# Four edits to a fused transformer and mixture-of-experts kernel: the order of its first two attentions, the router constants, the rotation rows, and the first norm of five batches

## The chip, the cores and the metric

The kernel runs on one core of one Trainium2 chip. A time is the device time of one execution in microseconds (us); medians are over several timed runs. The profile is of one further execution, taken by the hardware profiler. Engines are named as in the profile: PE is TensorE's matmul, PEld its weight load, DVE VectorE, ACT ScalarE, POOL GpSimd, SP SyncE.

## The reference

The input `x` is 8 batches of 256 tokens with 256 channels in float32; `cond_256` is a condition vector of 64 numbers for each batch, and `mask` a row of masked keys. Four layers follow, each added to its input:

```
# layer 0: attention with 16 heads, then a gated feed-forward of 1024 hidden channels
norm(x, t, ...) = (t @ gw.T + gb) * x * rsqrt(mean(x*x) + 1e-6) + (t @ bw.T + bb)
x1 = x + attention(norm1(x), Wq, Wk, Wv, Wo)
x  = x + x1 + (silu(norm2(x1) @ gate_w.T) * (norm2(x1) @ hid_w.T)) @ out_w.T
# layer 1: masked attention, then an RMS norm scaled and shifted by silu(cond) @ Wc.T + bc
x  = x + modulated_rmsnorm(masked_attention(x))
# layer 2: a spectral gate that is constant over frequency, then quaternion products: a 4x4 mix
#          for each of 64 positions of the channel group ("rotation")
x  = x + rotate(x * gate)
# layer 3: 8 experts of three matrices, the 2 best for each token, weighed by a softmax
gate = (rms_w * x * rsqrt(mean(x*x) + 1e-6)) @ wg_W + wg_b + (cond @ gg_W + gg_b)
x  = x + sum over the top 2 experts of weight * expert(x)
```

The factor and the offset of layer 0's norms depend on the batch and the channel alone, and the last bracket of the router's `gate` ("router constants") on the batch and the expert alone.

## The kernel before

A batch of 256 tokens lies as two tiles of 128 tokens; `NQ` is 2, and `KC` is the 2 chunks of 128 channels. The work of layers 0 and 1 runs batch by batch; the experts follow, in tiles of tokens that are gathered by expert.

**Order.** TensorE's instructions run in the order of the program's text throughout (`manual_schedule`), VectorE's and ScalarE's until the experts, GpSimd's during the first twelve attention blocks. SyncE, which issues most loads, is put in order by the framework's scheduler. A block (`block`) is one of an attention's four pieces: the scores of a chunk of heads `c` against a half of the keys `kc` (`s_a`, four matmuls over 32 rows), and one exponential on ScalarE (`pe_a`). There is one buffer of scores in PSUM, so the next scores wait for the exponential. Every second block also multiplies with the values (`values`, `o_a`); VectorE then turns the sums (`tu_a`), divides them and turns them again (`oT_a`). After the second such piece `after_first` projects them out (`py`, which reads `oT_a`), adds the input and starts the second norm.

`run` plays a string of blocks. Beside each block it takes pieces from a generator until the assumed costs reach the block's gap (a piece is 1.9 if it says nothing else; a "break" ends the block's pieces), calls what a finished attention has left over (`then`, after at most `soon` further pieces), and at the block's end one step of the generators given in `beside`. `others(b)` yields the feed-forward of batch `b` (`swiglu`: turns of the second norm, groups `pg` and `ph`, then `pd`), mixed with the first operands of batch `b + 3` (`first`) and the operands of its second attention. For batch 0 its first piece, the turns, is followed by a "break".

**First norm of a batch.** `first_norm` squares on ScalarE, takes the reciprocal root on VectorE in eleven small instructions (`rsqrt`), and multiplies the token-major rows on GpSimd (`xs_n`). `first` then has TensorE turn them (`flipped`, four transposes into `pt_n`), and VectorE evicts them with factor and offset (`xT_n`, through `conditioned`).

**Router constants.** `set_up_router` multiplies the condition, repeated for 128 rows, with `ggw`: one matmul of 8 columns for each batch (`pgconst`).

**Rotation.** `prepare_quaternions` normalizes and lays out the quaternions (VectorE, then 32 small copies on GpSimd into `lm` and `rm`), `prepare_rotation` multiplies them, `set_up_rotation` spreads the sixteen coefficients of each position over all partitions: diagonal matrices on VectorE (`diag`), two matmuls with ones (`pcoef`), copies on ScalarE (`coef`). It is a generator; `second_step` plays it in steps, one for each of five blocks.

**The head.** TensorE first multiplies the identity with itself (`keep_busy`, `pw`) while the first batch is loaded and squared. `set_up_factors(j0)` makes factors and offsets of a norm with eight small matmuls (`paff`); before, those of the first norm are made in the head and those of the second beside the first block.

PSUM tiles tagged "m" (projections, turns, `py`, feed-forward) share three banks.

Of the kernel before, what the change touches and what calls it, by code (L numbers as in the profile page):

```python
# [8 lines left out]
F32 = mybir.dt.float32  # L9
# [9 lines left out]
C = 64  # L19
# [474 lines left out]
def block_kernel(ctx: ExitStack, tc: tile.TileContext, a: dict, out: bass.AP):  # L494
# [10 lines left out]
    tokens_r = tokens[0:T, :].rearrange("(q p) c -> p q c", p=P)  # L505
    mod_rows = dram.tile([B, 2 * D], F32, tag="mod_rows", name="mod_rows")

    slots = dram.tile([TABLE, 4], I32, tag="slots", name="slots")
# [69 lines left out]
    first_factors, second_factors = slice(0, 2), slice(2, 4)  # L578
    nc.sync.dma_start(out=aff_w[:, first_factors, :], in_=a["aff_w"][:, first_factors, :])
    wk0 = load_w(nc.sync, "L0_WkT", D, D, pool_a)  # L580
# [4 lines left out]
    wo0 = load_w(nc.sync, "L0_WoT_turned", D, D, pool_a)  # L585
    nc.sync.dma_start(out=aff_w[:, second_factors, :], in_=a["aff_w"][:, second_factors, :])
    gate_w = load_w(nc.sync, "gate_wT", D, HID, pool_b)
# [158 lines left out]
    def prepare_router():  # L746
        cond_b = pool_b.tile([C, B, P], F32, tag="hT", bufs=1, name="cond_b")
        nc.vector.tensor_copy(cond_b, condT[0:C, :].unsqueeze(2).to_broadcast([C, B, P]))

        for k in range(KC):  # L750
            nc.vector.tensor_scalar(wgs[:, k, :], wg[:, k, :], rmsw[:, k : k + 1], None, ALU.mult)
        nc.vector.tensor_tensor(gb_b, wgb_b, ggb_b, ALU.add)
        nc.vector.tensor_copy(rank, ranki)
        return cond_b

    def set_up_router(cond_b):
        pg = ps_m.tile([P, B, E], F32, tag="m", name="pgconst")
        for b in range(B):
            nc.tensor.matmul(pg[:, b, :], cond_b[:, b, :], ggw, start=True, stop=True)
        nc.vector.tensor_tensor(gconst, pg, gb_b.unsqueeze(1).to_broadcast([P, B, E]), ALU.add)  # L760
        yield 0.4
# [35 lines left out]
    def set_up_rotation():  # L797
# [16 lines left out]

        diag = []
        for n in range(2):
            d = work.tile([C, 2, 4, C], F32, tag="x3", bufs=2, name=f"diag_{n}")
            for i in range(2):
                nc.vector.tensor_tensor(
                    d[:, i], ident[0:C, 0:C].unsqueeze(1).to_broadcast([C, 4, C]),  # L820
                    rotg[0:C, :, 2 * n + i : 2 * n + i + 1].to_broadcast([C, 4, C]), ALU.mult,
                )
            diag.append(d)
        yield
        for n in range(2):
            pc = bank(f"pcoef_{n}", (P, 2 * 4 * C))
            nc.tensor.matmul(
                pc, ones[0:C, :], diag[n].rearrange("p i j c -> p (i j c)"), start=True, stop=True
            )
            nc.scalar.copy(coef[:, 2 * n : 2 * n + 2], pc)  # L830

# [6 lines left out]
        )  # L838
        scaled = work.tile([P, KC, B, E], F32, tag="r_msg", bufs=1, name="scaled")
        nc.vector.tensor_tensor(  # L840
# [30 lines left out]
    def bank(name, shape=(P, 2, S)):  # L871
        return ps_m.tile(list(shape), F32, tag="m", name=name)
# [165 lines left out]
    def do(parts):  # L1038
        for _ in parts:
            pass  # L1040
# [5 lines left out]
    def first_norm(b):  # L1046
# [5 lines left out]
        )  # L1052

    def first(b):

        s = state[b]
        xT = conditioned(
            s.pop("xs1"), b, 0, f"n1_{b}", (nc.vector, nc.vector if b else nc.scalar), apart=b == 0
        )
        yield 0.6  # L1060
        s["qkv0"] = yield from qkv(xT, wq0, wk0, wv0, f"a0_{b}")
# [705 lines left out]

    def keep_busy(n, name):

        pw = bank(name, (P, P))  # L1770
        for _ in range(n):
            nc.tensor.matmul(pw, ident, ident, start=True, stop=True)

    by_text = {mybir.EngineType.DVE, mybir.EngineType.Activation, mybir.EngineType.Pool}
    with tc.manual_schedule(engines=by_text):
        keep_busy(9, "pw0")
        n1 = first_norm(0)
        next(n1)
        next(n1)
        set_up_factors(0)  # L1780
        do(n1)
        keep_busy(4, "pw1")
        g0 = first(0)
        next(g0)
        keep_busy(3, "pw2")
        scales()
        do(first_norm(1))
        for _ in g0:
            pass
        blank = set_up_slots()  # L1790
        prepare_condition()
        cond_b = prepare_router()
        finish_slots(*blank)
        def factors():
            set_up_factors(2)
            yield 0.4

        def third(b):

            operand = first(b)  # L1800
            yield next(operand)
            yield from set_up_router(cond_b)
            yield from operand

        operands = chain(set_up_condition(), factors(), first(1))
        run("b", operands, 1.4, rest=False)
        run("bbb", operands, 1.9, {1: [at_once(first_norm(2))]})
        operands = third(2)
        run("bb", operands, [1.0, 3.8], rest=False)

        def second_step():
            set_up_rows()
            prepare_quaternions()
            yield
            rotation = set_up_rotation()
            next(rotation)
            yield
            next(rotation)
            yield
            do(first_norm(3))  # L1820
            next(rotation)
            set_up_ones()
            yield
            yield from rotation

        set_up = second_step()
        run("bbbbbb", chain(operands, others(0)), 7.2, {n: [set_up] for n in range(5)})
    by_text = {mybir.EngineType.DVE, mybir.EngineType.Activation}
# [3 lines left out]
    for i in range(2, B - 1):  # L1832

        placed = {
            2: lambda: once(compare_queries), 4: lambda: at_once(place_choices(0)),
            6: lambda: at_once(place_choices(1)),
        }.get(i, lambda: iter(()))()
        last, rotated = rotated, rotate(i - 2)
        n1 = first_norm(i + 2) if i + 2 < B else iter(())
        n2, r1 = in_parts(i, "n2"), in_parts(i - 2, "r1")  # L1840
        gaps = [7.6, 5.7, 3.8, 5.7, 8.2, 3.8, 2.5, 3.8] if i + 2 < B else [7.6, 3.8, 1.9, 5.7, 7.6, 1.2, 1.9, 3.8]
        starts = {0: [last], 1: [last, n2], 2: [n2, n1]}
        beside = {
            0: [last], 1: [last, n2], 2: [n1, n1], 3: [last], 4: [placed], 5: [r1], 6: [rotated],
            7: [rotated, rotated],
        }
        if i == B - 2:

            early = table("early", (NG - 2) * NTG, EARLY, ALU.is_ge)
            for t in (4, 7):  # L1850
                beside[t].append(early)
        run("bbbbbbbb", others(i - 1), gaps, beside, late_=() if i + 2 < B else (4,), starts=starts)
# [12 lines left out]
    n2 = in_parts(B - 1, "n2")  # L1865
    run("bbbvn", pieces, 3.8, {0: [n2], 2: [early], 3: [early]}, soon=2, rest=False, starts={0: [n2], 1: [n2]})

# [192 lines left out]
```

## Time and profile before

| what | value |
|---|---|
| median of 3 timed runs | 710.83 us (710.71 to 712.07) |
| the profiled execution's own time | 712.39 us |
| its span, first to last instruction | 710.7 us |
| mean granted TensorE clock | 0.995 |
| busy share of PE, PEld, DVE, ACT, POOL | 98%, 76%, 52%, 36%, 26% |
| first scores of attention a0_0, a0_2, a1_0 | 16.46, 58.57, 99.38 us |
| TensorE's own idle time by the waits, 0 to 130 us | 1.5 us at the start, 0.4 later |

Lines of a timeline read: start, length, engine, line of the kernel, instruction, output and inputs, shape, how many in a row; in brackets the idle time before and what ended it. Lengths of matmuls overlap, since they are pipelined: the cost of a group in a row is the distance from its start to the next group's start. Lines of the windows read: stretch, its length, then busy time and number of instructions of PE, PEld, DVE, ACT and POOL, the granted clock of TensorE, the share of the DMA engines, and GB/s.

### The profile page before, as it was taken

The page shows a single profiled execution, that of the slowest core. Times are in us where ns is not written, and L with a number is a line of the kernel's source. Part 1 is how long each engine was busy: PE and PEld are TensorE (multiplying, and loading weights), DVE is VectorE, ACT ScalarE, POOL GpSimd, SP SyncE. Part 2 cuts the span into 40 slices and gives each one's busy share as a digit, 9 for nine tenths or more (in the row PEclk, how much of TensorE's full clock was granted, in tenths as well). Part 3 has the DMA queues.
Part 4 walks back from the last instruction along what each step waited for, and adds up shares of the span by engine and source line. Part 5 has one row for each costly group of instructions (what it writes and reads, how often), then busy time and mean ns, then how long its engine had stood idle before and what let it go on. Part 6 is the DMA issues. An engine that isn't in the chain of part 4 may idle for free.

```text
span 710.7 us, 11254 instructions
## 1 busy us (share of the span) xinstructions
PE 698.1 (98%) x4300; PEld 538.6 (76%) x4300; DVE 368.1 (52%) x1175; ACT 256.4 (36%) x412; POOL 182.2 (26%) x222
## 2 busy tenths in 40 slices
PE   9999999999999999999999999999999999999995
PEld 8567776766766767766666786788888998999894
DVE  4547445485477585477585686688421222222221
ACT  3653334354364354264444235422221212222120
POOL 5302500100100140100140016323464432352213
PEclk9999999999999999999999999999999999999999
DMA  8500000000011000001000050827675867586722
GB/s 284 177 17 0 16 1 16 1 16 16 1 56 35 1 17 1 0 21 54 2 17 1 16 201 11 305 88 242 155 251 159 251 224 220 152 262 206 247 32 30
DMA packets 26495, 67.52 MB, mean 95 GB/s; under 512 B 8056, under 2 KB 20608, under 8 KB 24000
## 3 DMA queue, kind: packets, MB, share of 16 engines
q1 hardware_dynamic: 17648, 55.20, 22.7%
q0 software_dynamic: 8496, 11.32, 7.4%
q8 instruction: 36, 0.59, 0.3%
q14 instruction: 27, 0.22, 0.1%
q10 hardware_dynamic: 288, 0.18, 0.1%
HBM read 57.18 MB, written 9.52 MB: 94 GB/s over the span
## 4 chain that ended last, share of the span: by engine, by line
PE 90%; DVE 6%; ACT 1%; issue 1%; POOL 0%; POOLq 0%; DVEq 0%; ACTq 0%
PE ph_a_rest L1495 10%; PE s_a L989 9%; PE o_a L1002 8%; PE ph_a_p L1495 7%; PE pd L1110 7%; PE pg L1097 7%; PE ph L1097 7%; PE ph_s_sure L1495 6%; PE pq_a L933 4%; PE pk_a L933 4%; PE pe_a_rest L1525 3%; PE pe_a_p L1525 3%; PE py L1025 2%; PE pe_s_sure L1525 2%; PE pv_a L963 2%; PE py L1143 2%
## 5 line engine op out<-in xcount | busy, mean ns | idle before, releaser
L991 ACT ACTIVATE pe_a<-s_a 128x2048 f32<-128x2048 f32 x64 | 120.1, 1877 | 106.9 <-PE s_a L989 106.7
L989 PE MATMUL s_a<-qz_a,kT_a 32*128 32x512 f32 x512 | 73.2, 639 | 0.6 <-ACT pe_a L991 0.2
L1097 PE MATMUL ph<-xT_n,hid_wT 128*128 128x256 f32 x256 | 61.7, 384 | 0.3 <-DVE sg L1103 0.3
L1097 PE MATMUL pg<-xT_n,gate_wT 128*128 128x256 f32 x256 | 61.9, 385 | 0.0
L1002 PE MATMUL o_a<-pe_a,va 128*32 128x256 f32 x1024 | 61.9, 382 | 0.0
L1002 PEld LDWEIGHTS o_a<-pe_a,va 128*32 128x32 f32 x1024 | 30.0, 109 | 39.9 <-issue 23.4
L1110 PE MATMUL pd<-out_wT,hT 128*128 128x256 f32 x256 | 59.2, 383 | 0.0
L1097 PEld LDWEIGHTS ph<-xT_n,hid_wT 128*128 128x128 f32 x256 | 47.6, 190 | 14.4 <-DVE y L1069 3.0
L1110 PEld LDWEIGHTS pd<-out_wT,hT 128*128 128x128 f32 x256 | 47.7, 190 | 12.3 <-issue 3.2
L1097 PEld LDWEIGHTS pg<-xT_n,gate_wT 128*128 128x128 f32 x256 | 47.4, 190 | 12.1 <-issue 2.5
L1495 PE MATMUL ph_a_rest<-h_a_rest,w_a_rest 128*128 128x256 f32 x224 | 49.6, 379 | 0.0
L1070 POOL TENSOR_TENSOR xy<-y,x 128x512 f32<-128x512 f32 x8 | 10.2, 1271 | 142.0 <-DVE y L1069 87.1
L1495 PEld LDWEIGHTS ph_a_rest<-h_a_rest,w_a_rest 128*128 128x128 f32 x224 | 42.0, 190 | 5.4
L1011 DVE STREAM_TRANSPOSE tu_a<-o_a 128x512 f32<-128x512 f32 x32 | 22.8, 712 | 39.8 <-PE o_a L1002 39.7
L1506 DVE TENSOR_SCALAR h_a_rest<-ph_a_rest,w_a_rest 128x256 f32<-128x256 f32 x28 | 13.5, 484 | 57.3 <-PE ph_a_rest L1495 56.3
L1283 POOL DMA_INDIRECT slots<-rec,posi x32 | 32.0, 1000 | 22.4 <-issue 7.9
L1495 PE MATMUL ph_a_p<-h_a_p,w_a_p 128*128 128x192 f32 (+2 forms) x224 | 36.0, 319 | 0.0
L1101 ACT ACTIVATE th<-pg 128x512 f32<-128x512 f32 x32 | 19.0, 595 | 45.1 <-PE pg L1097 44.5
L1504 ACT ACTIVATE h_a_rest<-ph_a_rest,w_a_rest 128x256 f32<-128x256 f32 x28 | 13.3, 474 | 60.6 <-DVE h_a_rest L1506 60.6
L1495 PEld LDWEIGHTS ph_a_p<-h_a_p,w_a_p 128*128 128x128 f32 x224 | 34.9, 191 | 0.1
L989 PEld LDWEIGHTS s_a<-qz_a,kT_a 32*128 32x128 f32 x512 | 20.2, 183 | 18.7 <-issue 12.8
L1103 DVE SCALAR_TENSOR_TENSOR sg<-th,pg 128x512 f32<-128x512 f32 x32 | 21.9, 683 | 23.9 <-ACT th L1101 23.9
(353 smaller groups left out, 1202.5 us busy)
## 6 DMA issues: line engine op xcount, KB each, us to landing
w_a_rest<-in_experts SPq DMA_DIRECT2D x7, 2180.0 KB, 9.3
w_a_p<-in_experts SPq DMA_DIRECT2D x7, 2180.0 KB, 9.5
w_s_sure<-in_experts SPq DMA_DIRECT2D x4, 2180.0 KB, 9.3
w_s_early<-in_experts SPq DMA_DIRECT2D x1, 2180.0 KB, 9.2
mod<-mod_rows SPq DMA_DIRECT2D x8, 256.0 KB, 3.2
tokens<-x SPq DMA_DIRECT2D x4, 512.0 KB, 3.3
out<-x SPq DMA_DIRECT2D x4, 512.0 KB, 4.5
x<-in_x SPq DMA_DIRECT2D x7, 256.0 KB, 2.7
```

What stands on the lines that cost most here:

```text
L933: nc.tensor.matmul(pp[:, c, :], w[:, k, c * P : (c + 1) * P], xT[:, k, :], start=k == 0, stop=k == KC - 1)
L989: nc.tensor.matmul(sc[:, j], kT[r, c, kc * P : (kc + 1) * P], qz[r, c], start=True, stop=True)
L991: nc.scalar.activation(pe, sc, AF.Exp)
L1002: nc.tensor.matmul(o[32 * i : 32 * i + 32, qd, :], va[:, kc, 8 * c + 4 * qd + i].rearrange("p a d -> p (a d)"), pe[:, 2 * qd + i // 2, i % ...
L1011: nc.vector.transpose(turned.rearrange("p q j a d -> p (q j a d)"), o.rearrange("p q s -> p (q s)"))
L1097: nc.tensor.matmul(ps[:, j, :], w[:, k, o : o + P], yT[:, k, :], start=k == 0, stop=k == KC - 1)
L1101: nc.scalar.activation(th, pg, AF.Tanh, scale=0.5)
L1103: nc.vector.scalar_tensor_tensor(sg, th, 1.0, pg, ALU.add, ALU.mult)
L1110: nc.tensor.matmul(pd[:, t, :], hT[:, c, t * P : (t + 1) * P], out_w[:, c, :], start=c == 0, stop=c == HID // P - 1)
L1283: sc = nc.gpsimd.indirect_dma_start(out=slots, out_offset=bass.IndirectOffsetOnAxis(ap=posi[:, t : t + 1], axis=0), in_=rec[:, t, :], in_o ...
L1495: nc.tensor.matmul(ph[:, c - c0, 0:many], w[:, o : o + P], src[:, k, 0:many], start=k == 0, stop=k == n_in - 1,)
L1525: nc.tensor.matmul(pos[q][0:p, q, :], h2[:, k, q * p : (q + 1) * p], w[:, o : o + D], start=k == 0, stop=k == MC - 1,)
```

## The change

1. *Order.* The factors of both norms are made in the head, and `keep_busy` is shortened there from 9, 4 and 3 to 9, 3 and 2. The first six blocks are called one by one with their own pieces, and the six after them have gaps of their own.
2. *Router constants.* VectorE multiplies condition and `ggw` element by element; one matmul with ones sums over the 64 conditions.
3. *Rotation rows.* The sixteen coefficients of each position are written to DRAM and read back by all partitions; ScalarE copies them into place. `diag` and `pcoef` are gone.
4. *First norm of batches 3 to 7.* `first_turned` loads a channel-major copy of the batch, laid out by the host (`xT`), writes the reciprocal roots to DRAM and reads them back as rows for all partitions. VectorE multiplies by them, GpSimd applies factor and offset. Its first step comes two blocks earlier in the loop.

The last loop before the experts also has `soon=3` for `soon=2`, and `scaled` moves to another buffer.

```diff
-    nc.sync.dma_start(out=aff_w[:, first_factors, :], in_=a["aff_w"][:, first_factors, :])
+    for js in (first_factors, second_factors):
+        nc.sync.dma_start(out=aff_w[:, js, :], in_=a["aff_w"][:, js, :])
...
     def prepare_router():
-        cond_b = pool_b.tile([C, B, P], F32, tag="hT", bufs=1, name="cond_b")
-        nc.vector.tensor_copy(cond_b, condT[0:C, :].unsqueeze(2).to_broadcast([C, B, P]))
+        cond_g = pool_b.tile([C, B, E], F32, tag="hT", bufs=1, name="cond_g")
+        nc.vector.tensor_tensor(
+            cond_g, condT[0:C, :].unsqueeze(2).to_broadcast([C, B, E]),
+            ggw.unsqueeze(1).to_broadcast([C, B, E]), ALU.mult,
+        )
...
-        for b in range(B):
-            nc.tensor.matmul(pg[:, b, :], cond_b[:, b, :], ggw, start=True, stop=True)
+        nc.tensor.matmul(
+            pg.rearrange("p b e -> p (b e)"), ones[0:C, :], cond_g.rearrange("c b e -> c (b e)"),
+            start=True, stop=True,
+        )
...
-        diag = []
...
-        yield
-        for n in range(2):
-            pc = bank(f"pcoef_{n}", (P, 2 * 4 * C))
...
-            nc.scalar.copy(coef[:, 2 * n : 2 * n + 2], pc)
+        nc.sync.dma_start(out=coef_row, in_=rotg[0:C].rearrange("c j i -> c (j i)"))
+        rows_in = wt("x4", [P, C, 4, 4], "coef_in", 1)
+        nc.sync.dma_start(
+            out=rows_in.rearrange("p c j i -> p (c j i)"),
+            in_=coef_row.rearrange("c w -> (c w)").partition_broadcast(P),
+        )
+        yield
+        nc.scalar.copy(coef, rows_in.rearrange("p c j i -> p i j c"))
...
+    def first_turned(b):
+        s = state[b]
+        s["x"] = xs_in.pop(b)
+        ss = squares(s["x"], f"n1_{b}")
+        xT = wt("xs", [P, KC, S], f"xr_{b}", 3)
+        nc.sync.dma_start(out=xT, in_=a["xT"][b])
+        yield
+        rstd = rsqrt(work, ss, NQ, 1.0 / D, 1e-6, f"n1_{b}")
+        nc.sync.dma_start(out=rstd_rows[b], in_=rstd)
+        rows_ = wt("rb", [P, P, NQ], f"rb_{b}", 1)
+        nc.sync.dma_start(
+            out=rows_.rearrange("p t q -> p (t q)"),
+            in_=rstd_rows[b].rearrange("t q -> (t q)").partition_broadcast(P),
+        )
+        yield
+        parts = xT.rearrange("p k (q t) -> p k q t", q=NQ)
+        nc.vector.tensor_tensor(
+            parts, parts, rows_.rearrange("p t q -> p q t").unsqueeze(1).to_broadcast([P, KC, NQ, P]), ALU.mult
+        )
+        dst = s["xT1"] = wt("xT", [P, KC, S], f"xT_n1_{b}", 3)
+        for k in range(KC):
+            nc.gpsimd.tensor_scalar(
+                dst[:, k, :], xT[:, k, :], aff[:, 0, k, b : b + 1], aff[:, 1, k, b : b + 1], ALU.mult, ALU.add
+            )
+        yield
...
     def first(b):
         s = state[b]
+        if "xT1" in s:
+            yield 0.6
+            s["qkv0"] = yield from qkv(s.pop("xT1"), wq0, wk0, wv0, f"a0_{b}")
+            return
...
         set_up_factors(0)
+        set_up_factors(2)
         do(n1)
-        keep_busy(4, "pw1")
+        keep_busy(3)
         g0 = first(0)
         next(g0)
-        keep_busy(3, "pw2")
+        keep_busy(2)
...
-        operands = chain(set_up_condition(), factors(), first(1))
-        run("b", operands, 1.4, rest=False)
-        run("bbb", operands, 1.9, {1: [at_once(first_norm(2))]})
-        operands = third(2)
-        run("bb", operands, [1.0, 3.8], rest=False)
+        operands = first(1)
+        run("b", chain(take(1, operands), set_up_condition(), set_up_router(cond_g)), 9.0, rest=False)
+        run("b", take(1, operands), 9.0, {0: [at_once(first_norm(2))]}, rest=False)
+        run("b", iter(()), 0.0)
+        run("b", operands, 9.0, rest=False)
+        operands = first(2)
+        then = run("b", iter(()), 0.0, hold=True)
+        run("b", take(1, operands), 9.0, owed=then, soon=1, rest=False)
...
             rotation = set_up_rotation()
             next(rotation)
             yield
+            n1 = first_turned(3)
+            next(n1)
+            next(n1)
             next(rotation)
             yield
-            do(first_norm(3))
+            do(n1)
             next(rotation)
             set_up_ones()
             yield
             yield from rotation
         set_up = second_step()
-        run("bbbbbb", chain(operands, others(0)), 7.2, {n: [set_up] for n in range(5)})
+        gaps = [1.9, 4.0, 7.2, 7.2, 7.2, 7.2]
+        run("bbbbbb", chain(operands, others(0)), gaps, {n: [set_up] for n in range(5)})
...
-        n1 = first_norm(i + 2) if i + 2 < B else iter(())
+        n1 = first_turned(i + 2) if i + 2 < B else iter(())
...
-        starts = {0: [last], 1: [last, n2], 2: [n2, n1]}
+        starts = {0: [last, n1], 1: [last, n2], 2: [n2]}
         beside = {
-            0: [last], 1: [last, n2], 2: [n1, n1], 3: [last], 4: [placed], 5: [r1], 6: [rotated],
+            0: [last, n1], 1: [last, n2], 2: [n1], 3: [last], 4: [placed], 5: [r1], 6: [rotated],
             7: [rotated, rotated],
         }
...
+        "xT": v["x"].transpose(0, 2, 1).reshape(B, KC, P, S).transpose(0, 2, 1, 3),
```

`take(n, pieces)` yields the next `n` pieces.

## The prediction

> **What bounds the kernel now.** I read the page first, then the TensorE timeline, the windows of two microseconds, and for the setup the timeline of all engines. The page: TensorE is busy for 98% of the span, and the chain that ended last is 90% TensorE.
>
> ```profile
> span 710.7 us, 11254 instructions
> PE 698.1 (98%) x4300; PEld 538.6 (76%) x4300; DVE 368.1 (52%) x1175; ACT 256.4 (36%) x412; POOL 182.2 (26%) x222
> ```
>
> So a matmul taken out anywhere is worth its full time, as long as TensorE still has something ready. Work moved to VectorE, GpSimd or a DMA is free only while TensorE has cover for it. The next lines (TensorE's timeline: start, length, then the group) show what is taken out and one stall that "busy" hides.
>
> ```profile
> 5.65 1.87 PE L634 MATMUL paff<-small_in,aff_w 64*128 64x8 f32 x8
> 7.45 2.07 PE L1772 MATMUL pw<-ident 128*128 128x128 f32 x8
> ...
> 18.55 1.06 PE L634 MATMUL paff<-small_in,aff_w 64*128 64x8 f32 x8
> ...
> 34.78 1.95 PE L759 MATMUL pgconst<-small_in,cond_b 64*128 64x8 f32 x16
> 36.84 2.43 PE L933 MATMUL pk_a<-xT_n,L_WkT 128*128 128x256 f32 x8
> 39.06 3.16 PE L1025 MATMUL py<-L_WoT_turned,oT_a 128*128 128x256 f32 x8
> 42.15 1.14 PE L989 MATMUL s_a<-qz_a,kT_a 32*128 32x512 f32 x8
> ...
> 68.61 1.98 PE L827 MATMUL pcoef<-diag,ones 64*128 64x512 f32 x4
> 70.43 0.95 PE L834 MATMUL pmc<-silu_c,WcT 64*128 64x8 f32 x8
> ```
>
> From start to next start, eight matmuls of 256 columns usually take 1.8 us; here `py` takes 3.09 and the `pk` before it 2.22. The windows say why: the granted clock (the 0.55 and 0.60) fell.
>
> ```profile
> 38.00:40.00 2.00, 2.00 (x7) 1.61 (x6) 0.00 (x0) 0.59 (x1) 0.00 (x0) 0.55 0.00 0
> 40.00:42.00 2.00, 2.00 (x7) 1.46 (x5) 0.00 (x0) 0.00 (x0) 0.00 (x0) 0.60 0.00 0
> ```
>
> That is about 0.4 + 1.3 = 1.7 us lost, right after two microseconds of the router's 8-column matmuls. The last view is the quaternion setup, which VectorE must do in text order ahead of the attention's own work:
>
> ```profile
> 51.94 0.15 DVE L679 TENSOR_TENSOR sq<-small_in 128x8 f32<-128x8 f32 x1
> ...
> 55.04 0.18 POOL L777 COPY lm<-pm 128x1 f32<-128x1 f32 x1 [10.32 <-DVE pm L684]
> ...
> 58.92 0.18 POOL L779 COPY rm<-pm 128x1 f32<-128x1 f32 x1
> ...
> 59.28 0.17 DVE L784 TENSOR_TENSOR rot<-lm,rm 128x16 f32<-128x16 f32 x1
> ...
> 62.24 1.41 DVE L819 TENSOR_TENSOR diag<-ident,rotg 64x256 f32<-64x256 f32 x4
> 63.58 0.70 DVE L1011 STREAM_TRANSPOSE tu_a<-o_a 128x512 f32<-128x512 f32 x1
> ```
>
> `tu_a` could have read its sums at 61.6, where `o_a` ended; it stood behind `rot` and `diag`. TensorE lost nothing, because three feed-forward groups of 1.8 us lay between `o_a` and the `py` that needs it.
>
> **What is taken off TensorE** (start to next start). Router constants: 34.78 to 36.84 is 2.06 us; one matmul of 64 columns remains, 0.25 by the `phall` rows (eight of 128x64 in 0.93): -1.8. Rotation rows: 68.61 to 70.43: -1.8. Turns of batches 3 to 7 at 83.44, 128.81, 182.41, 236.06 and 290.88: 0.49, 0.53, 0.53, 1.38 (0.6 of it waiting for GpSimd's `xs`) and 0.53, together -3.5; `pk` at 86.00 also waited 0.2 for the eviction. The slow clock after the router: -1.7. The second `paff` at 18.55 leaves for the head: -1.0. Sum: -10.0.
>
> **What the new norm costs.** VectorE gives up two evictions (0.50 each) for one product of 512 (0.69, the `y` row); GpSimd keeps two passes of 0.92. SyncE gets three more issues per batch, in the queue that also loads `x` and `mod` and has waited 40 us for a buffer. The round trip through DRAM has a row: `mod_rows` was issued at 23.24, its reader at 27.07 and that lands 3.2 later, 7.0 us in all. Two blocks, some 13 us (163.0 to 176.1 in batch 2's loop), lie between the reciprocal root and its product in the loop: I cost it at nothing. If a wait heads the queue, VectorE stands at the product with the evictions behind it, up to 6 us once; if there is no wait, VectorE gains 0.3 per batch that nobody needs. The rotation rows make the same trip with less cover: from `rotg` to ScalarE's copy I count 8 us (`gall` 1.3, `tu` to `oT` 1.95, `py_1` 1.9, `y` 0.7, squares 2.2), against 7.0.
>
> **The head.** Eight more `paff` matmuls stand ahead of the first transposes. At 5.65 eight took 1.80, at 18.55 0.99. I take 1.8, being at the same place, less 0.47 for a `keep_busy` and 0.1 for another: +1.2 (+0.4 at the faster rate). The matmuls ran slow until about 10.9, after a full stretch of `pw`; this stretch now starts 1.8 later, so `pk` and `pq` of batch 0 would run partly slow: +0.9 (0 to 1.7).
>
> On such slow stretches the Trainium skill, "TensorE: Matmul & The Clock Gate", section "What's actually happening", gives windows of about 3.4 us after which the array's clock is halved or restored, and warns of idle gaps of that length. The rows agree in length (about 38.2 to 41.6), but here the array was not idle, only fed with 8-column matmuls; by the rule alone the router's stretch would have cost nothing, and the sum would be 1.7 higher.
>
> **The order of the first two attentions.** A block with too little beside it lasts 3.13 us from scores to scores (20.13 to 23.26: scores 1.2, exponential 1.88). Following the new calls: block 1 has the turns, `pmod` and the router (2.9), block 2 `pk` (2.9), block 3 only `o` (2.9, and the exponential stands 0.5 behind the squares of batch 2), block 5 only `o`. These wait 0.4, 0.2, 0.6 and 0.2, and `py_0` 0.4 for its `oT`: 1.8, where the old order waited about 1.0. +0.8.
>
> Now the six blocks with gaps 1.9, 4.0, 7.2. The first takes `pk_2`, the second `pq_2`, `pv_2` and the turns of the second norm (1.9 + 1.9 + 0.6 reaches 5.9). The third begins with the "break" that follows these turns, and has batch 1's `after_first` in hand: `py_1` follows `o` at once, with none of the seven feed-forward groups ahead of it. What must be done between `py_0` and `py_1`, one after another: `y` 0.7, squares 1.1, reciprocal root 2.15, `tu` to `oT` 1.95, quaternions 3.15, GpSimd's copies 4.1, rotation up to `gall` 3.05, `tu` to `oT` 1.95, hand-overs 0.3: 18.4 us. TensorE has between them three scores (3.2), two `o` (3.7), three projections (5.4) and turns (0.6): 12.9. It is short by 5.5 us: 1.3 ahead of a0_2's scores, since `qz_2` stands behind the quaternions, and 4.1 in one piece ahead of `py_1`. Bounds: 2.1 if the rotation were done in time (then only `tu` to `oT` shows), 6 if the copies take longer. A piece of 4 us without matmuls is more than the 2.06 that cost the clock before: +1.7 again (0 to 3.4). After `py_1`, `mc` stands on VectorE behind two reciprocal roots of 2.1 and holds one of three PSUM banks: the third feed-forward group waits 1.3 (0 to 1.5).
>
> Queued behind later waits I find nothing more: in the loop's first block the moved root delays `hT` by 2.1, and at 222.5 its bank has 2.8 us to spare. `soon=3` near 445 swaps equal pieces: 0 (-0.3 to 0.3).
>
> **Sum.** -10.0 + 1.2 + 0.9 + 0.8 + 5.5 + 1.7 + 1.3 = +1.4 us, against the profiled execution's 712.39 (span 710.7 and 1.7 around it). The median is 710.83, 1.56 lower, nearly a slow clock's 1.7: in such runs that 1.7 may not be there to gain, which would make it +3.1. Between them I take +1.7, near the profiled row: 712.5. A measurement here tells about 0.2% (1.4 us) from no change.
>
> **Rivals.** (a) *The hole is covered*: if `tu` is not held by the rotation, or feed-forward groups stand ahead of `py_1`, 5.5 and 1.7 drop out: +1.4 - 7.2 = -5.8, about 705. The saturated TensorE speaks for it; that VectorE kept `diag` ahead of `tu` at 63.58 speaks against. It decides once less than about 2 us is missing at `py_1`. (b) *The hole is there but the clock holds*, as the clock held elsewhere in the first 36 us with small waits: -0.3, about 710.7, no change. (c) *The rotation rows land late*, and ScalarE's copy holds the exponentials behind it: 4 us more, about 716.5. (d) That the norm is slow in the loop: covered above, at most 6 us, counted with (c).
>
> **How the numbers follow.** Forecast 0.50, its own range 711 to 714.5, by the head (0.4 to 2.9) and the clock; it is slower by over 0.2% in 0.42 and inside in 0.08. (a) 0.25, all faster. (b) 0.20: 0.14 inside, 0.06 faster. (c, d) 0.05, slower. So faster 0.31, same 0.22, slower 0.47. The range runs from (a) at 705.0 to 715.0; (c) and deeper gains stay out.
>
> **What would show it.** Right: pt_n with no turns for first norms of batches 3 to 7, no `pcoef`, one short `pgconst`; `pk` of batch 0 near 12.4; TensorE idle 3 to 5 us ahead of `py` of batch 1, released by VectorE's `oT`, then a granted clock near 0.5 for 3 us; no hole in the loop. Wrong: `py_1` following within 1 us of its `o`, or a head that starts `pk` by 11.2; then the time is near (a).

## The result and the profile after

The changed kernel takes 709.7 us (median of 12 runs, 708.12 to 714.73), the kernel before, run beside it, 710.77 (12 runs, 708.42 to 712.53). The ratio is 0.9997 with a 95% interval of 0.9975 to 1.0019: no change that can be told. A second comparison on another chip gave 0.9996 (0.9972 to 1.002). The profiled execution took 708.63 us. The page of the changed kernel says:

```profile
span 706.9 us, 11183 instructions
PE 687.8 (97%) x4258; PEld 529.6 (75%) x4258; DVE 367.2 (52%) x1166; ACT 257.2 (36%) x411; POOL 178.7 (25%) x222
```

TensorE has 10.3 us less to do than before (698.1), but the span is only 3.8 shorter. That 10.3 is close to the 10.0 which the prediction took off is in part chance: about 2.1 of it come from the head, whose matmuls ran faster in this execution although there are more of them. TensorE's timeline shows where it now waits. (Columns as before; brackets hold the idle time ahead and what ended it.)

```profile
5.21 1.95 PE L636 MATMUL paff<-small_in,aff_w 64*128 64x8 f32 x16
...
15.47 1.14 PE L988 MATMUL s_a<-qz_a,kT_a 32*128 32x512 f32 x8 [1.11 <-DVE half_c L695]
...
18.08 0.43 PE L763 MATMUL pgconst<-cond_g,ones 64*128 64x64 f32 x2
...
47.44 1.14 PE L988 MATMUL s_a<-qz_a,kT_a 32*128 32x512 f32 x8 [1.01 <-DVE qz_a L946]
...
50.37 0.70 PE L1024 MATMUL py<-L_WoT_turned,oT_a 128*128 128x256 f32 x2
53.93 1.56 PE L1024 MATMUL py<-L_WoT_turned,oT_a 128*128 128x256 f32 x6 [2.85 <-DVE oT_a L1018]
...
61.77 1.99 PE L1128 MATMUL pg<-xT_n,gate_wT 128*128 128x256 f32 x8 [0.57 <-DVE mc L834]
64.10 1.10 PE L847 MATMUL phall<-scaled,wo1n 128*128 128x64 f32 x8 [0.34 <-DVE sg L1134]
```

The parts do what they say: 16 `paff` in the head, one short `pgconst` of two matmuls, no `pcoef`, no turns for the first norms of batches 3 to 7. The hole is where the prediction put it: the scores of a0_2 wait 1.01 for `qz_a`, and `py` of batch 1 stops after two matmuls and waits 2.85 for VectorE's `oT_a`. VectorE and GpSimd in that stretch:

```profile
45.51 0.19 POOL L784 COPY lm<-pm 128x1 f32<-128x1 f32 x1 [6.59 <-DVE pm L686]
...
48.78 0.17 DVE L791 TENSOR_TENSOR rot<-lm,rm 128x16 f32<-128x16 f32 x1 [1.49 <-POOL lm L784]
...
51.94 0.71 DVE L1010 STREAM_TRANSPOSE tu_a<-o_a 128x512 f32<-128x512 f32 x1
...
53.43 0.45 DVE L1018 STREAM_TRANSPOSE oT_a<-on_a 128x256 f32<-128x256 f32 x1
```

`rot` waits 1.49 for GpSimd's copies, and `tu_a`, whose sums `o_a` were complete at 50.4, starts at 51.94, when the rotation is done. What did not come in this execution is the slow clock. The windows across the hole (stretch, length, then busy time of each engine, and the granted clock as the third number from the end):

```profile
52.00:54.00 2.00, 0.07 (x1) 0.07 (x1) 1.77 (x5) 0.00 (x0) 0.00 (x0) 1.00 0.22 31
56.00:58.00 2.00, 2.00 (x15) 1.18 (x15) 0.75 (x4) 1.59 (x7) 1.27 (x1) 1.00 0.00 0
```

The loop has a new wait that the prediction had ruled out, 0.42 at `pd` of the first block of a batch, behind the moved reciprocal root:

```profile
230.51 2.86 PE L1141 MATMUL pd<-out_wT,hT 128*128 128x256 f32 x12 [0.42 <-DVE hT L1136]
```

The difference of the two profiled executions (spans 710.7 and 706.9) is made up so: first scores 16.46 to 15.47, -1.0; from there to the first scores of a1_0 82.92 to 81.28, -1.6; the turns of batches 4 to 7 -0.44, -0.44, -0.64 and -0.43, together -1.95; +0.2 between 364 and 440; +0.6 from GpSimd's last scatter (703.17 before, 698.79 now) to the end of the span. Sum -3.8. The first two of these are mostly a matter of which execution was profiled: the first profile of the kernel before has a slow clock behind the router, and in a second one without it (`before_again`) the same stretch takes 81.24 us, so that the changed kernel's 81.28 is no gain there.

### The profile page after: what moved, and what is told of

It reads as the page before. It is cut to its first block, busy times and chain, and to the rows that moved or that the text cites. A ratio compares the mean times of both kernels' runs of the same rounds, so it can differ in the third digit from the quotient of the medians.

```text
span 706.9 us, 11183 instructions
## 1 busy us (share of the span) xinstructions
PE 687.8 (97%) x4258; PEld 529.6 (75%) x4258; DVE 367.2 (52%) x1166; ACT 257.2 (36%) x411; POOL 178.7 (25%) x222
## 4 chain that ended last, share of the span: by engine, by line
PE 83%; DVE 8%; ACT 1%; issue 1%; POOL 1%; POOLq 0%; DVEq 0%; ACTq 0%
PE ph_a_rest L1526 10%; PE pd L1141 8%; PE ph_a_p L1526 7%; PE s_a L988 7%; PE o_a L1001 7%; PE pg L1128 6%; PE ph L1128 6%; PE ph_s_sure L1526 6%; PE pe_a_rest L1556 3%; PE pk_a L932 3%; PE pq_a L932 3%; PE pe_a_p L1556 3%; PE pe_s_sure L1556 2%; PE pv_a L962 2%; PE py L1174 2%; PE py L1024 2%
## 5 line engine op out<-in xcount | busy, mean ns | idle before, releaser
L1526 PE MATMUL ph_a_rest<-h_a_rest,w_a_rest 128*128 128x256 f32 x224 | 49.6, 379 | 0.0
L1101 POOL TENSOR_TENSOR xy<-y,x 128x512 f32<-128x512 f32 x8 | 10.2, 1272 | 138.3 <-DVE rq_v_n L619 57.5
L1537 DVE TENSOR_SCALAR h_a_rest<-ph_a_rest,w_a_rest 128x256 f32<-128x256 f32 x28 | 13.5, 484 | 57.3 <-PE ph_a_rest L1526 56.3
```

What stands on the lines that cost most here:

```text
L1526: nc.tensor.matmul(ph[:, c - c0, 0:many], w[:, o : o + P], src[:, k, 0:many], start=k == 0, stop=k == n_in - 1,)
```

## The experiments

Eight of the twelve runs below came to chips on which every kernel, the one before too, took 3% longer (before: medians of 735.51 and 733.57 us; in the last set 710.70). So each ratio is against runs of the kernel before on the same chip, and within the profiles two stretches are compared: from the start to the first scores ("head"), and from these to the first scores of a1_0 ("first attentions"), in which the changed order lies.

| kernel | head | first attentions | ratio to before, 95% interval |
|---|---|---|---|
| before; `before_again` | 16.46; 17.65 | 82.92; 81.24 | 1 |
| after; `after_again` | 15.47; 18.26 | 81.28; 83.02 | 0.9997; 0.9996 |
| `e1_break_first` | 18.42 | 77.56 | 0.9945 (0.9918 to 0.9973) |
| `e2_old_order` | 14.48 | 81.39 | 0.9965 (0.9943 to 0.9987) |
| `e3_norm_only` | 14.28 | 80.38 | 0.9952 (0.9930 to 0.9974) |
| `e4_order_only` | 15.37 | 93.06 | 1.0106 (1.0057 to 1.0155) |
| `e5_steps_later` | 15.54 | 79.03 | 0.9957 (0.9932 to 0.9981) |
| `e6_filled_hole` | 18.42 | 84.46 | 1.0025 (1.0003 to 1.0048) |
| `e6b_filled_less` | 15.82 | 81.53 | 0.9986 (0.9970 to 1.0001) |
| `e7_break_head` | 15.04 | 80.01 | 0.9923 (0.9895 to 0.9952) |
| `e8_break_later` | 15.54 | 78.40 | 0.9938 (0.9916 to 0.9960) |
| `e9_break_head_later` | 14.99 | 79.23 | 0.9946 (0.9927 to 0.9965) |

### Is the hole the break? (`e1_break_first`)

```diff
-        gaps = [1.9, 4.0, 7.2, 7.2, 7.2, 7.2]
+        gaps = [1.9, 4.7, 7.2, 7.2, 7.2, 7.2]
```

With 4.7 the second block takes up the "break" as well, so the third block begins with feed-forward.

> The changed kernel with one number changed: the second of the six gaps is 4.7 instead of 4.0, so that the break after the turns is used up in the second block and three feed-forward groups (5.3 us) come between o_a and py of batch 1. Theory H (the rotation holds VectorE and leaves TensorE a hole ahead of py): the idle 2.9 to 3.6 us ahead of py goes, the wait of 0.6 for mc may go too, the wait of 1.0 for qz_2 stays; 3 to 4.5 us faster than the changed kernel (709.7), so 705 to 707, and a granted clock of 0.995 or more in most runs. Rival G (the loss is given back elsewhere: whatever fills the hole here is missing later): within 1 us of the changed kernel.

TensorE's timeline of this kernel where the hole was:

```profile
53.33 1.99 PE L1128 MATMUL pg<-xT_n,gate_wT 128*128 128x256 f32 x8
...
56.89 1.89 PE L1128 MATMUL pg<-xT_n,gate_wT 128*128 128x256 f32 x8
58.62 1.89 PE L1024 MATMUL py<-L_WoT_turned,oT_a 128*128 128x256 f32 x8
```

Three groups of feed-forward stand ahead of `py`, and it no longer waits. VectorE's chain is the same to 0.2 us: `rot` still waits 1.47 for the copies, and its `oT` starts at 56.37, 2 us ahead of `py`. The first attentions take 77.56 us, 3.72 less than in the changed kernel; the 1.01 at `qz_a` stays. So theory H holds: one number in a list of gaps is worth half a per cent of the kernel (0.9945 against 0.9997 and 0.9996).

### The parts alone (`e2_old_order`, `e3_norm_only`, `e4_order_only`)

`e2_old_order` is the changed kernel with the head and the calls of the first twelve blocks of before, and `soon=2`:

```diff
-        set_up_factors(2)
...
-        run("b", chain(take(1, operands), set_up_condition(), set_up_router(cond_g)), 9.0, rest=False)
...
+        operands = chain(set_up_condition(), factors(), first(1))
+        run("b", operands, 1.4, rest=False)
+        run("bbb", operands, 1.9, {1: [at_once(first_norm(2))]})
...
-        gaps = [1.9, 4.0, 7.2, 7.2, 7.2, 7.2]
-        run("bbbbbb", chain(operands, others(0)), gaps, {n: [set_up] for n in range(5)})
+        run("bbbbbb", chain(operands, others(0)), 7.2, {n: [set_up] for n in range(5)})
```

> The changed kernel with the order of the kernel before in the head and in the first twelve blocks (and soon=2); router constants, rotation rows and the new norm stay off TensorE. Theory H: only the order costs, so what was taken off TensorE shows: 1.8 (router) + 1.8 (rotation) + 2.2 to 2.7 (turns), 5.5 to 6.5 us below the kernel before, near 704.5, and faster than the changed kernel by some 5. No fall of the granted clock near 38 us, since the router's stretch is gone. Rival N (the round trips through DRAM cost what the matmuls gave): within 1.5 us of the kernel before. Rival O (the new order is what gains): slower than the changed kernel.

`e3_norm_only` is the kernel before with `first_turned` alone:

```diff
+    def first_turned(b):
+        ...
-        n1 = first_norm(i + 2) if i + 2 < B else iter(())
+        n1 = first_turned(i + 2) if i + 2 < B else iter(())
```

> The kernel before with the new first norm of batches 3 to 7 alone (scaled sits in the mod buffer as in the changed kernel, for room). Theory H: 0.44 to 0.64 us for each of five batches, 2.2 to 2.7 us faster, near 708.3; the slow clock near 38 us still appears in some runs. Rival N: the same as before or slower, with VectorE waiting for the rows of reciprocal roots.

`e4_order_only` is the kernel before with the changed head and calls:

```diff
-        run("bbbbbb", chain(operands, others(0)), 7.2, {n: [set_up] for n in range(5)})
+        gaps = [1.9, 4.0, 7.2, 7.2, 7.2, 7.2]
+        run("bbbbbb", chain(operands, others(0)), gaps, {n: [set_up] for n in range(5)})
```

> The kernel before with the new order alone: router constants by eight matmuls, rotation rows by diagonal matrices and matmuls, first norms turned on TensorE. Theory H: the hole ahead of py of batch 1 is 1.4 us longer than in the changed kernel (the diagonal matrices stand ahead of tu_a too), about 5 us; 2 to 6 us slower than the kernel before, 713 to 717. Rival O: faster than the kernel before by 1 to 3 us.

Against the kernel before, `e2_old_order` gained 2.5 us where 5.5 to 6.5 were expected, `e3_norm_only` 3.5 where 2.2 to 2.7 were (its interval, 0.26% to 0.70%, takes them in), and `e4_order_only` lost 10 where 2 to 6 were.

`e2_old_order` and `e3_norm_only` differ in the router constants and the rotation rows (and `soon` is 2 in both). With these two edits TensorE has 3.4 us less to do in the first attentions, and the kernel is no faster: 733.02 against 731.97 us, and 81.39 against 80.38 in the first attentions. TensorE's timeline of `e2_old_order`, then that of `e3_norm_only`, at the place of the router:

```profile
32.74 0.43 PE L763 MATMUL pgconst<-cond_g,ones 64*128 64x64 f32 x2
34.80 3.14 PE L932 MATMUL pk_a<-xT_n,L_WkT 128*128 128x256 f32 x8 [1.63 <-DVE xT_n L924]
37.73 2.45 PE L1024 MATMUL py<-L_WoT_turned,oT_a 128*128 128x256 f32 x8
...
74.05 2.86 PE L1141 MATMUL pd<-out_wT,hT 128*128 128x256 f32 x12 [0.84 <-DVE hT L1136]
```

```profile
32.60 1.95 PE L760 MATMUL pgconst<-small_in,cond_b 64*128 64x8 f32 x16
34.67 1.96 PE L934 MATMUL pk_a<-xT_n,L_WkT 128*128 128x256 f32 x8
```

In `e3_norm_only` the sixteen router matmuls fill the 2 us in which VectorE turns the sums of batch 0 and evicts the operand of batch 2, and `pk_a` follows at once. In `e2_old_order` they are gone, and `pk_a` waits 1.63 for that eviction; in this execution the clock fell to 0.5 behind the wait (35.4 to 38.9), and `pk_a` and `py` cost 2.93 and 2.38 instead of 1.80 and 1.82. Without `pcoef`, `pd` comes up to the feed-forward's `hT` and waits 0.84. So in the old order both were cover for something else: the two waits take back 2.5 of the 3.4 us, and the slow clock, which need not come in each execution, another 1.7. In `e1_break_first`, with the new order and no hole, they pay: 77.56 against 80.38. The norm alone, in `e3_norm_only`, gives about as much as that whole kernel (0.9952); its turns, 0.49 for batch 3 and the 1.95, explain 0.33% of it. The rest may be the clock, which held behind the router in this profile and did not in the first one of before; that was not tested, and the interval alone leaves room for it.

`e4_order_only` is the worst of all, and its times spread from 737.84 to 748.60. Its hole is longer, 4.19, since `diag` (1.41) stands ahead of `tu_a` too. The lines behind it, and a window:

```profile
59.42 2.93 PE L1025 MATMUL py<-L_WoT_turned,oT_a 128*128 128x256 f32 x6 [4.19 <-DVE oT_a L1019]
62.28 3.78 PE L827 MATMUL pcoef<-diag,ones 64*128 64x512 f32 x4
```

```profile
62.00:64.00 2.00, 2.00 (x3) 0.83 (x3) 0.69 (x1) 0.80 (x3) 0.83 (x1) 0.50 0.00 0
```

`pcoef` takes 3.58 to the next start where it took 1.82 before. The clock is at 0.5 from 57.2 to 70.9, and once more from 19.7 to 26.5, behind the router matmuls that this order puts between two scores. So the new order without the other parts costs 12 us in the first attentions (93.06 against 81.24), in this execution most of it clock: from start to start, the groups in the two slow stretches take some 8 us more than the same groups elsewhere.

### Does the clock fall behind the hole? (`after_again`, `e6_filled_hole`, `e6b_filled_less`)

`after_again` has no edit.

> The changed kernel once more, unaltered, beside the same runs of the kernel before as the next three, so that ratios of one chip can be compared. Theory (a hole of some 3 us ahead of py of batch 1, and in a part of the executions a halved clock behind it): ratio 0.996 to 1.002; executions spread over 5 us or more, and if this profile shows the granted clock at 0.5 behind the hole, its span is 3 to 6 us over a profile that does not show it. Rival (the clock has nothing to do with the hole): the slow stretch, if there is one, lies anywhere else.

Its profile shows the same waits of 1.00 and 2.84, and this time the slow clock. TensorE's timeline and a window:

```profile
56.70 1.63 PE L1024 MATMUL py<-L_WoT_turned,oT_a 128*128 128x256 f32 x6 [2.84 <-DVE oT_a L1018]
58.26 1.87 PE L833 MATMUL pmc<-silu_c,WcT 64*128 64x8 f32 x8
60.06 2.09 PE L988 MATMUL s_a<-qz_a,kT_a 32*128 32x512 f32 x8
62.08 3.37 PE L1128 MATMUL pg<-xT_n,gate_wT 128*128 128x256 f32 x8
```

```profile
58.00:60.00 2.00, 2.00 (x10) 1.75 (x8) 0.69 (x1) 0.82 (x3) 0.86 (x1) 0.52 0.10 39
```

`pmc` takes 1.80 to the next start (0.99 in the first profile), the scores 2.02 (1.07), `pg` 3.20 (1.83). The first attentions last 83.02 instead of 81.28: +1.74 for the same program and the same hole. The slow stretch itself costs more, 3.2 us: from the second part of `py` to `ph` it is 8.58 here and 5.38 in the first profile. But the waits for `mc` and `sg` behind it are gone, since TensorE now comes later than VectorE, and that gives 1.4 back. Of its 12 runs five have a mean clock of 0.975 to 0.978 (median 733.8), seven 0.980 to 0.988 (median 732.19).

The fill puts matmuls that nobody reads into the hole:

```diff
+        if b == 1:
+            fill = bank("fill", (P, P))
+            for _ in range(24):
+                nc.tensor.matmul(fill, ident, ident, start=True, stop=True)
         py = outward(oT, wo0, f"py_{b}")
```

> The changed kernel with 24 matmuls of 128 columns, whose result nobody reads, ahead of py of batch 1 (24 x 0.115 = 2.8 us), so that TensorE is fed while it waits for VectorE's oT. Nothing that is computed changes and VectorE's chain is the same. Theory that the hole costs twice, by its idle time and by the clock: the idle time stays lost (scores to scores of the first batch's two attentions about 81.3 to 81.7 us, as in the changed kernel), but no slow clock follows it in any execution, so the median is 0 to 2 us under the changed kernel's and the upper end of its executions comes down by some 3 us. Rival that only the idle time counts: median and spread as the changed kernel's, within 1 us.

The size was wrong: each call in float32 is two matmuls in the profile, so the fill lasted 5.46 us, `py` came at 58.78 instead of 56.7 or so, and the kernel is slower. It still shows one thing: on the chip of `after_again`, all its 12 runs have a clock of 0.981 to 0.985. With 12 calls the fill fits:

> As the kernel with the filled hole, but with 12 calls: in the first version each call became two matmuls (48 in the profile, 5.46 us, longer than the hole itself), so that half of them fits (24 matmuls, 2.7 us). Theory that an idle TensorE is what halves the clock: the idle time ahead of py falls under 1 us, py itself comes at most 0.4 us later than in the changed kernel, no slow clock follows (pmc 1.0, the scores behind it 1.07, pg 1.83 from start to start), scores to scores of the first batch 81.3 to 81.9 us where the unfilled one had 81.3 without and 83.0 with the slow clock; ratio 0.997 to 1.000. Rival that the slow clock comes anyway: 83 us in part of the executions.

```profile
50.71 2.94 PE L1100 MATMUL fill<-ident 128*128 128x128 f32 x24
...
54.25 1.56 PE L1024 MATMUL py<-L_WoT_turned,oT_a 128*128 128x256 f32 x6 [0.16 <-DVE oT_a L1018]
```

The wait at `py` is 0.16, the clock stays at 1.00, the first attentions last 81.53. Ten of 12 runs lie between 708.08 and 709.60, two at 711.6 and 711.9; of the changed kernel's twelve on the first chip seven lie below 709.8 and five between 711 and 714.8. Of the filled kernel's runs 11 have a mean clock of 0.995 or more, of the changed kernel's six. So filling a hole with idle work gains none of the hole, and it fits the theory that fewer executions are then followed by a slow clock. It is not shown: two long runs against five, on different chips, can be chance, and the unfilled kernel, too, has one profile without a slow clock. Where the last two of 12 come from was not shown either.

### What holds VectorE, and what the head costs (`e5_steps_later`, `e7_break_head`, `e8_break_later`, `e9_break_head_later`)

```diff
-        run("bbbbbb", chain(operands, others(0)), gaps, {n: [set_up] for n in range(5)})
+        run("bbbbbb", chain(operands, others(0)), gaps, {n: [set_up] for n in range(1, 6)})
```

> The changed kernel with the steps of the second set-up (rows and quaternions, rotation, turned norm) each one block of scores later. The theory says that py of batch 1 and the scores of batch 2 wait for VectorE because the quaternions and the rotation stand ahead of their oT and qz in VectorE's order: then the wait of 1.0 at qz of batch 2 goes, and of the 2.9 at py at most 2.1 is left (tu to oT alone); what is late next is mc and gall, 1 to 2 us in the fourth block. Scores to scores of the first batch 78.5 to 80.5 us instead of 81.3; ratio to the changed kernel 0.996 to 0.999. Rival that the text order doesn't matter and py waits for the o sums alone: the hole stays at 2.9 and the time with it.

As the theory said: `qz_a` no longer waits, `py` waits 1.45 instead of 2.85, and a new wait of 1.26 stands at `pmc` (behind the `sg` of feed-forward, with the rotation ahead of it on VectorE). With `e1_break_first` this shows the cause of the hole from both sides: it goes when TensorE has other work there, and it shrinks when VectorE's rotation comes later. The first attentions take 79.03, and the ratio is 0.4% lower than that of `after_again`.

```diff
-        set_up_factors(2)
...
+        def factors():
+            set_up_factors(2)
+            yield 0.4
...
-        run("b", chain(take(1, operands), set_up_condition(), set_up_router(cond_g)), 9.0, rest=False)
+        run("b", chain(set_up_condition(), factors(), take(1, operands), set_up_router(cond_g)), 9.0, rest=False)
...
-        gaps = [1.9, 4.0, 7.2, 7.2, 7.2, 7.2]
+        gaps = [1.9, 4.7, 7.2, 7.2, 7.2, 7.2]
```

> The changed kernel with the gap of its second block of six at 4.7 instead of 4.0 (the break then falls one block later, and three feed-forward groups stand ahead of py of batch 1), and with the second half of paff back in the first block behind the scores, its load back behind the weights, as before the change. Theory that the two costs are independent: the gap is worth 3.7 us in the first attentions (77.6 us instead of 81.3), the head 1.0 us where the clock starts early and 2.0 where it starts late, less 1.0 for paff in the block: 4 to 5 us under the changed kernel, ratio to the kernel before 0.992 to 0.994, first scores at about 14.4 or 16.5. Rival that the head was covered anyway: as the gap alone, 3.7 us.

The ratio is the expected one, 0.9923, but the profile says it is hardly the head: the first scores come at 15.04 instead of 14.4, since they wait 0.49 for VectorE, and the first attentions take 80.01 instead of 77.6. The eight small matmuls in the first block are followed by a clock of 0.5 from 19.5 to 22.9 (4.64 us from the scores behind them to the next, in place of 3.14 in `e9_break_head_later`, where the same eight stand and the clock holds). `e8_break_later` joins the gap of `e1_break_first` and the later steps:

> The changed kernel with both: gap 4.7 in the second block, and the second set-up's steps one block later. Theory that the two repair different waits: the gap covers py (3.7 us), the later steps take the 1.0 at qz of batch 2 as well, and rot no longer waits for GpSimd's copies; scores to scores of the first batch 76.4 to 77.0 us, ratio to the kernel before 0.992 to 0.9945. Rival that mc and the sg of feed-forward, now late behind the rotation, take it back: 77.5 or more, as with the gap alone (77.6).

```profile
64.24 1.99 PE L1128 MATMUL pg<-xT_n,gate_wT 128*128 128x256 f32 x8 [1.26 <-DVE hT L1136]
```

The first attentions take 78.40, so the rival was right: the waits at `qz_a` and `py` are gone, but the rotation now stands ahead of the second and third `hT`, `pg` waits 1.26 for it, and later `pv_a` 0.67 for `x2T`. The kernel takes 705.51 us (705.14 to 708.22), 0.6% under the kernel before. `e9_break_head_later` adds the old place of the second `paff`:

> The three together: gap 4.7, steps one block later, and the second half of paff in the first block as before the change. By the sum of the parts 0.7 us under the gap and the head alone: ratio to the kernel before 0.991 to 0.993. Against it: in the profile with paff in the first block 8 small matmuls more lay between scores there, and the clock fell to 0.5 from 19.2 to 22.5 (1.7 us); where that happens in this kernel too, it is no better than the version without the head.

706.56 us: 0.55 gained in the head and 0.83 lost in the first block, so nothing. Of the kernels with all four parts, five lie 0.4 to 0.8% under the one before, and their intervals overlap; the smallest edits among them are the gap of `e1_break_first` and the later steps of `e5_steps_later`.

> The kernel before, unaltered, for a profile beside the last runs, whose times are all some 3% over those of the first runs. If that belongs to the chip and not to the edits, this profile has the same three waits of 3 to 5 us at pv_a, pv_a and pk_a of batches 4, 6 and 7, which the first profile of the kernel before does not have, and a time of 730 to 738. Scores to scores of the first batch is 81.2 us, or 82.9 if the clock falls behind the router as it did in the first profile.

This run came to a chip of the first kind (711.77 us), so the question of those three waits stays open. It answers the other one: the router's matmuls, at 35.97 here, cost no clock, and the first attentions last 81.24, 1.68 under the first profile of the kernel before.

## Why the prediction was right, and where not

**The mechanism came, the forecast time did not.** The forecast was 712.5 us, slower than before; measured are 709.7, 1.1 under the kernel before and no change that can be told. That is the result of rival (b), priced at 710.7. The hole came where it was forecast, with `oT` of VectorE as releaser and the rotation ahead of `tu_a`; the first profile shows rival (b), the clock that holds, and the second the forecast's slow clock. A choice between "clock falls" and "clock holds" was the wrong form of the question: both are the same program, whose twelve runs spread from 708.12 to 714.73.

**The slow clock's size was right by luck.** Assumed were 1.7 us, measured 1.74. But the stretch lasts 6.8 us, not 3, and costs 3.2; the 1.4 that come back are the waits for `mc` and `sg`, which the prediction added on top as 1.3. An execution pays one of the two, not both. And the 1.7 that the change was to gain behind the router is there only where the clock falls: in `before_again` it held.

**The hole was mis-sized.** 5.5 was predicted as 18.4 us of chain less 12.9 of TensorE's work; measured are 1.01 and 2.85, together 3.86. From the end of `py` of batch 0 (36.34) to the second part of `py` of batch 1 (53.93) it is 17.6, so the chain was 0.8 too long. These 0.8 are an overlap: the prediction put the rotation behind all of GpSimd's copies, but `rot` starts at 48.78, and the last copy ends at 49.6. The rest is that two of `py`'s eight matmuls (0.5) run ahead of the hole, and that its other work took 0.3 longer. `mc` and the `sg` behind it cost 0.57 and 0.34 instead of 1.3. These terms alone are 2.0 us. The prediction's terms for the first attentions (-7.0 and +9.3) make 85.2 us with a slow clock; `after_again`, which has it, shows 83.02.

**The head** was to cost 2.1 by TensorE's own work. The windows show a granted clock of 1.00 in the whole head, but its matmuls run at two paces: the sixteen `paff` take 1.87 us in the first profile of the changed kernel and 3.51 in the second. Where the pace rises late, the prediction's way of counting holds: `after_again` starts `pk` at 12.29, where 12.4 was forecast, and its first scores come at 18.26, against 16.46 and 17.65 before (and at 18.42 in `e1_break_first`), so the head costs 0.6 to 2.0. Where it rises early, they come at 14.28 and 14.48 with the old head and at 15.37 to 15.82 with the new one, 0.9 to 1.5 later, and this cost is of another kind. ScalarE and VectorE in the first profile:

```profile
10.40 0.42 ACT L878 ACTIVATE junk_n<-x 128x256 f32<-128x256 f32 x1 [1.29 <-DMA x<-in_x]
...
13.92 1.40 DVE L946 TENSOR_SCALAR qz_a<-pq_a,par 128x512 f32<-128x512 f32 x2
```

The first scores read `qz_a`, not `half_c`, which is only what VectorE finished last. `qz_a` stands on VectorE behind the reciprocal root of batch 1, this waits for ScalarE's squares, and these for the load of batch 1. In all eight profiles in which the squares wait for that load, the first scores come 5.06 or 5.07 us after the squares start. They start at 10.30 to 10.75 in the five early-paced profiles with the new head, in which the second half of `aff_w` (128 KB) stands ahead of that load in the text, and at 9.41 to 9.97 in the three with that half behind it. That this load order is the cause fits, but no run moved it alone. That the profile before has the late pace and the profile after the early one makes -1.0 out of a cost.

**The turns of batches 4 to 7** gave 1.95 instead of 2.97: each turn 0.44 instead of 0.53, and the 1.38 of batch 6 only 0.64, since the moved reciprocal root holds up `hT` and `pd` waits 0.42. The prediction had named this delay and found 2.8 us to spare at one `hT`; the wait came at the `pd` behind a later one. This step and the head were wrong in kind, not in size.

**The norm and the rotation rows** cost almost nothing, as predicted: VectorE waits for the returned roots once, 3.5 us for batch 3, and nobody behind it is late; the rotation rows landed at 56.3, 2 us ahead of ScalarE's copy, so rival (c) did not come. But the copy takes 1.92, and with the squares ahead of it it holds the exponential and the feed-forward's `th` behind it:

```profile
58.35 1.92 ACT L829 COPY coef<-coef_in 128x1024 f32<-128x1024 f32 x1
```

The exponential starts at 60.18, although its scores were done by 57.5, and `th` at 62.75. VectorE's `sg` waits 1.11 for `th`, and `phall` 0.34 for `sg`. The 0.34 would go without the copy, by these rows; no run tried it.

**Rival (a)**, at 705, was the right price, to 2 us, for the kernel without the hole: its condition, feed-forward groups ahead of `py`, is the edit of `e1_break_first`, and with it the kernels lie 0.55% (3.9 us) to 0.6% (705.5 us) under the kernel before. The removed 10 us are worth 4 to 5 then. The rest went into the head, the turns' hand-overs and waits that the removed matmuls had covered, and 1.7 of it was a slow clock that many executions do not have; no run divides it further.

## What to carry to other kernels

A matmul is worth its time only if what stands behind it is ready earlier: before taking small work off a full engine, look for the eviction that it covers. Where several pieces on another engine must come between two matmuls, add them up in that engine's order and compare with the first engine's work in between; if it is short, move ready work ahead of the wait before anything else. And where the clock falls in some executions only, profile the same kernel twice before a step is blamed.

## What the runs showed of the hardware

Every slow stretch that the windows show between the head and the last experts lasts 3.4, 6.8 or 13.7 us, one, two or four times the same length: 38.2 to 41.6 (before), 35.4 to 38.9 (`e2_old_order`), 58.1 to 64.9 (`after_again`), 19.6 to 26.5 and 57.2 to 70.9 (`e4_order_only`). The same hole of 2.85 us was followed by one in one execution and by none in another; so were the router's 2 us of 8-column matmuls (before against `before_again`). The Trainium skill, "TensorE: Matmul & The Clock Gate", section "What's actually happening", says that the window is free-running and about 3.4 us long, which fits both the lengths and the chance. Its idle window of that length as the condition does not fit: an idle time of 1.63 us was enough (`e2_old_order`), and one of 2.84 (`after_again`); in `e4_order_only` the clock fell 2.0 us into the idle time of 4.19; and behind the router's 2 us of 8-column matmuls it fell with no idle time at all.

On the chips where all kernels took 3% longer, each of the eight profiles has three waits of TensorE in the loop, of 1.1 to 4.7 us. VectorE stands still for 3.3 to 7.9 us there and ScalarE for 5.9 to 7.7, beside GpSimd's scatters to `slots`, and a slow stretch goes with each. The largest of them in the waits view of `e3_norm_only` (line, what it waited for, total, times, longest):

```profile
PE pv_a L964 <- DVE xT_n L926: 4.7, 1, 4.7
```

What holds the two engines there was not found, and no profile of the kernel before on such a chip was taken.
